# The chunked layer's preparation in a fixed order, with two blocks of its convolution on the tensor engine

## The chip, the core and the metric

The kernel runs on one core of a Trainium2 chip. A core has five engines that take their instructions from queues of their own: PE (TensorE: matrix products), DVE (VectorE), ACT (ScalarE) and POOL (GpSimd) for element-wise work, and SP (SyncE), which here only issues DMAs. PE writes to PSUM, a small memory that DVE and ACT read; everything else works on SBUF. The metric is the device time of one launch in microseconds (us); lower is better.

## The reference

Eight images of 64 x 64 x 96 in fp32 pass through four layers, each as `x = x + layer(group_norm(x))`. Layers 0 and 2 are selective scans, layer 3 upsamples, transforms and filters spectrally, and layer 1, which the change concerns, is a scan in chunks:

```python
xz = x @ in_proj_w.T                       # 96 -> 2 x 192
xi, z = split(xz)
u = silu(depthwise_conv3x3(xi, conv_w) + conv_b)
xs = cross_scan(u)                         # k = 0: by rows, 1: by columns, 2 and 3: both reversed
dt_raw, B, C = split(x_proj_w[k] @ xs[k])  # 6 + 16 + 16 rows for each direction k
dt = softplus(dt_raw + dt_bias[k])
# for each chunk of positions: decays exp(cumsum(dt * A)), C.B within the chunk, a state between chunks
y = cross_merge(scan(xs, dt, A, B, C, D))
x_out = layernorm(y) * silu(z) @ out_proj_w.T
```

The 192 channels of u are the six heads of 32; the scan needs, for every position, u with positions on the partitions, dt, B in two layouts and C.

## The kernel before

The loop over images (line 1566) runs, for each image, group norm, the input projection and the layer's own function for layers 0, 1 and 2; `back` (line 303) does the gate, norm and output projection of one layer at the start of the next. The spectral layer of an image is executed in small pieces beside the next image's two selective scans, and for the last image alone at the end. No such pieces run beside the chunked layer.

Activations have channels on the partitions: `y` (the projection's output) and `u` (after convolution and silu) are 96 x 2 halves x 4096 positions.

`chunked_scan` (line 1036) loads the layer's constants and calls `chunked_order` (line 1072) twice: with `o = 0` for the directions 0 and 2 (positions row by row) and with `o = 1` for 1 and 3 (column by column). Each call has two parts. The second part is a loop over 32 chunks of 128 positions in both directions (lines 1172 to 1422), written under `tc.manual_schedule()`: the order in the program is the order in each engine's queue. The first part is the preparation (lines 1086 to 1170). It has no such mark, so a list scheduler orders its instructions on each engine by their dependencies. It consists of:

- for `o = 0` alone, the convolution. Seven of the eight blocks of eight rows are done on DVE (`conv`, line 275: nine taps, lines 280 and 282), in portions of rows 0-16, 16-32, 32-48 and 48-56, each for two halves of the channels; block 7 is done on PE with diagonal matrices (`conv_pe`, line 291, matrices made by POOL in `diagonals`). Each portion ends with ACT's activation (`silu`, line 296), which writes `u`.
- `pr`: the B and C rows for all positions (line 1117). One tile holds four groups of 512 positions for one direction; there are four tiles. DVE copies each from PSUM to `bcs` (line 1125) and four DMAs of SP's queue write it to DRAM (`bcd`, line 1128), from where the loop's `quad` reads it back as `bt` and `cr` for four chunks at a time.
- for each of 32 chunks, a tile `pt` (three PSUM buffers): two matmuls, one for each half of the channels, give the transposed u of that half and the half's share of two directions' dt rows and B rows (line 1143). With `o = 1` a chunk's positions lie 64 elements apart, and each half is first copied together into `uc` (four buffers): half 0 by POOL (line 1137), half 1 by ACT (line 1138). The transposed u goes to `xt` (line 1144), by ACT in even and by DVE in odd chunks; ACT copies half 0's 44 small columns to `xd` (line 1148) and DVE adds those of half 1 (line 1149).
- at the end, for all chunks together: dt with its bias (line 1153), softplus (line 1158), the decays' factors `lw` and the ends of chunks (to line 1170).

The loop's first instructions on DVE include a memset of a PSUM tile, `pst2` (line 1186).

Of the kernel before, what the change touches and what calls it, by code (L numbers as in the profile page):

```python
# [9 lines left out]
F32 = mybir.dt.float32  # L10
# [7 lines left out]
DM = 96  # L18
NST = 16
RK = 6  # L20
# [7 lines left out]
Q = 128  # L28
NQ = L // Q
# [38 lines left out]
def tile_vision_stack(  # L68
# [19 lines left out]
    nc = tc.nc  # L88
# [60 lines left out]
    with (  # L149
# [6 lines left out]
        for i, (dtw, dtx, w) in enumerate(((dt0, dx0, w0), (dt2, dx2, w2))):  # L156
# [12 lines left out]
            for k in range(K):  # L169
                pw = pp.tile([DM, 2, 192], F32, name="pw", bufs=2)  # L170
                for hf in range(2):
# [4 lines left out]
                        start=True,  # L176
                        stop=True,
# [12 lines left out]
        for m in range(3):  # L190
            pt = pp.tile([128, DM], F32, name="pt")
# [71 lines left out]
    def taps(y, rows, hf, acc):  # L263

        at, end = rows
        av = acc.rearrange("p (r c) -> p r c", c=64)
        xv = y[:, hf, :].rearrange("p (r c) -> p r c", c=64)
        for tap in (4, 0, 1, 2, 3, 5, 6, 7, 8):
            dy, dx = tap // 3 - 1, tap % 3 - 1
            r0, r1 = max(at, -dy), min(end, 64 - dy)  # L270
            c0, c1 = max(0, -dx), min(64, 64 - dx)
            src = xv[:, r0 + dy : r1 + dy, c0 + dx : c1 + dx]
            yield tap, src, av[:, r0 - at : r1 - at, c0:c1]

    def conv(w, y, u, rows, hf):
        out = u[:, hf, rows[0] * 64 : rows[1] * 64]
        for tap, src, dst in taps(y, rows, hf, out):
            cw = w[:, C_CW + hf * 9 + tap : C_CW + hf * 9 + tap + 1]
            if tap == 4:
                nc.vector.tensor_scalar_mul(dst, src, cw)  # L280
            else:
                nc.vector.scalar_tensor_tensor(dst, src, cw, dst, ALU.mult, ALU.add)
        silu(w, u, rows, hf, out)

    def diagonals(dg, w):
        for n in range(18):
            nc.gpsimd.tensor_scalar_mul(
                dg[:, n, :], ident[:DM, :DM], w[:, C_CW + n : C_CW + n + 1]
            )

    def conv_pe(dg, y, j, hf, acc):
        for tap, src, dst in taps(y, (8 * j, 8 * j + 8), hf, acc):
            nc.tensor.matmul(dst, dg[:, 9 * hf + tap, :], src, start=(tap == 4), stop=(tap == 8))

    def silu(w, u, rows, hf, acc):
        nc.scalar.activation(
            u[:, hf, rows[0] * 64 : rows[1] * 64],
            acc,
            AF.Silu,
            bias=w[:, C_CB + hf : C_CB + hf + 1],  # L300
        )
# [119 lines left out]
    def view(t, wh, at, n):  # L421

        if not wh:
            return t[:, at : at + n]
        return t.rearrange("p (h w) -> p w h", w=64)[:, at // 64 : (at + n) // 64, :]

    def cut(t, wh):

        return t.rearrange("p (w h) -> p w h", h=64) if wh else t
# [260 lines left out]
    def selective_scan(w, wdt, a, d, u, y, beside):  # L690
# [23 lines left out]
        with (  # L714
# [14 lines left out]
            def prepare(i):  # L729

                k, c = steps[i]
                wh, at = k % 2 == 1, c * LC
                uv = [view(u[:, hf, :], wh, at, LC) for hf in range(2)]
                m = made[i] = {"dx": [], "du": []}
                if i in (0, 2, NCH + 2, 2 * NCH + 2):
# [336 lines left out]
    def chunked_order(o, w, d, xproj, u, y, yr, cc, lw, bts, crs, bcds, op):  # L1072
# [8 lines left out]
        xt = op.tile([128, NQ, 192], F32, name="xt")  # L1081
        xd = op.tile([128, NQ, 2, RK + NST], F32, name="xd")
        dt = op.tile([128, NQ, 2, RK], F32, name="dt")
        TX = DM + 2 * (RK + NST)
        d_end = op.tile([128, NQ, 2, RK], F32, name="d_end")
        with (
            tc.tile_pool(name="turn", bufs=2) as cp,
            tc.tile_pool(name="pt", bufs=3, space=PSUM) as ptp,
            tc.tile_pool(name="pc", bufs=1, space=PSUM) as pcp,
            tc.tile_pool(name="pr", bufs=2, space=PSUM) as prp,  # L1090
            tc.tile_pool(name="acc", bufs=2, space=PSUM) as acp,
        ):
            if o == 0:
                dg = cp.tile([DM, 18, DM], F32, name="dg", bufs=1)
                diagonals(dg, w)
                for rows in ((0, 16), (16, 32), (32, 48), (48, 56)):
                    for hf in range(2):
                        conv(w, y, u, rows, hf)
                for hf in range(2):
                    acc = acp.tile([DM, 512], F32, name="acc")  # L1100
                    conv_pe(dg, y, 7, hf, acc)
                    silu(w, u, (56, 64), hf, acc)
            tx = cp.tile([DM, 2, TX], F32, name="tx", bufs=1)
            for hf in range(2):
                nc.gpsimd.tensor_copy(tx[:, hf, :DM], ident[:DM, :DM])
                nc.gpsimd.tensor_copy(
                    tx[:, hf, DM:].rearrange("p (i r) -> p i r", i=2),
                    xproj[:, o::2, hf, : RK + NST],
                )

            for j in range(2):
                for i in range(2):
                    k = o + 2 * i
                    pr = prp.tile([128, 4 * Q], F32, name="pr")
                    for hf in range(2):
                        for g in range(4):
                            nc.tensor.matmul(
                                pr[32 * g : 32 * g + 32, :],
                                xproj[:, k, hf, RK:XR],
                                view(u[:, hf, :], o == 1, (4 * j + g) * 4 * Q, 4 * Q),  # L1120
                                start=(hf == 0),
                                stop=(hf == 1),
                            )
                    bcs = cp.tile([128, 4 * Q], F32, name="bcs")
                    nc.vector.tensor_copy(bcs, pr)
                    for g in range(4):
                        at = (4 * j + g) * 4 * Q
                        nc.sync.dma_start(
                            bcds[k][:, at : at + 4 * Q], bcs[32 * g : 32 * g + 32, :]
                        )  # L1130
            for c in range(NQ):
                if o == 0:
                    uv = [u[:, hf, c * Q : (c + 1) * Q] for hf in range(2)]
                else:

                    uc = cp.tile([DM, 2, Q], F32, name="uc", bufs=4)
                    nc.gpsimd.tensor_copy(cut(uc[:, 0, :], True), view(u[:, 0, :], True, c * Q, Q))
                    nc.scalar.copy(cut(uc[:, 1, :], True), view(u[:, 1, :], True, c * Q, Q))
                    uv = [uc[:, hf, :] for hf in range(2)]

                pt = ptp.tile([128, 2, TX], F32, name="pt")
                for hf in range(2):
                    nc.tensor.matmul(pt[:, hf, :], uv[hf], tx[:, hf, :], start=True, stop=True)
                (nc.vector.tensor_copy if c % 2 else nc.scalar.copy)(
                    xt[:, c, :].rearrange("p (j m) -> p j m", j=2), pt[:, :, :DM]
                )
                xdc = xd[:, c, :, :].rearrange("p i r -> p (i r)")
                nc.scalar.copy(xdc, pt[:, 0, DM:])
                nc.vector.tensor_add(xdc, xdc, pt[:, 1, DM:])
            for i in range(2):  # L1150
                k = o + 2 * i
                bias = r1s[:, k * RK : (k + 1) * RK]
                nc.vector.tensor_add(
                    dt[:, :, i, :],
                    xd[:, :, i, 0:RK],
                    bias.unsqueeze(1).to_broadcast([128, NQ, RK]),
                )
            nc.scalar.activation(dt, dt, AF.Softplus)
            for i in range(2):
                k = o + 2 * i  # L1160
                a = r1s[:, 24 + k * RK : 24 + (k + 1) * RK]
                dt_a = lw[:, i, :, RK : 2 * RK]
                nc.vector.tensor_mul(
                    dt_a, dt[:, :, i, :], a.unsqueeze(1).to_broadcast([128, NQ, RK])
                )

                pe = pcp.tile([128, NQ, RK], F32, name="pe")
                nc.tensor.matmul(pe, past[i], dt_a, start=True, stop=True)
                nc.scalar.activation(d_end[:, :, i, :], pe, AF.Exp)
            nc.vector.tensor_mul(d_end, d_end, dt)  # L1170
# [395 lines left out]
    for b in range(batch):  # L1566
        xd = xp.tile([DM, L], F32, name="xd")
# [7 lines left out]
        with tc.tile_pool(name="layers", bufs=1) as uyp:  # L1575
            u = uyp.tile([DM, 2, L], F32, name="u")
            y = uyp.tile([DM, 2, L], F32, name="y")
            stats = uyp.tile([DM, 8, 6], F32, name="stats")
            sbs = [uyp.tile([DM, 2], F32, name=f"sb{n}") for n in range(3)] + [sb3]
            for n in range(4):  # L1580
                with (
# [3 lines left out]
                    if n == 0:  # L1585
                        wi = columns(rp, w0, W_IN, 192, "wi")
                        xs = rp.tile([DM, L], F32, name="xs")
                        with (
# [11 lines left out]
                            for j in range(8):  # L1600
                                pt = pp.tile([DM, 4, 128], F32, name="pt")
# [170 lines left out]
```

## Time and profile before

| | us |
|---|---|
| median of 3 runs | 27056.74 |
| lowest and highest | 27053.37, 27074.89 |
| profiled execution, its own time | 27082.74 |
| its span on the core | 27080.9 |
| DVE busy in the span | 23966.2 (88%) |
| PE busy | 22624.0 (84%) |
| POOL busy | 21781.7 (80%) |
| ACT busy | 16539.7 (61%) |
| first preparation of image 0, from the projection's first matmul to line 1153 | 1400.46 to 1505.91 |
| second preparation of image 0, from its first matmul to line 1153 | 1701.19 to 1736.84 |

Times in the profile count from the start of the span. A row of the timeline gives start and duration, the engine, the line, the operation, what it writes and reads, partitions x elements, how many instructions the row holds together, and in brackets how long the engine had been idle and what released it. A matmul in fp32 shows as two records. PEclk is the share of the full clock that the tensor engine was granted.

### The profile page before, as it was taken

To read this page: it belongs to the slowest core of one execution; us is meant where nothing else is said; L and a number is where in the kernel's file an instruction comes from. 1 tells how busy PE (TensorE), PEld (TensorE's weight loads), DVE (VectorE), ACT (ScalarE), POOL (GpSimd) and SP (SyncE) were. 2 spreads that over 40 slices of the span, in tenths; PEclk is the share of its full clock that TensorE was granted. 3 is DMA by queue.
4 is the path that set the end of the run, shared out by engine and by line. 5 is a ranking of instruction groups with operands and counts; after the bars stand their busy time and mean duration, and the time that the engine had idled before them with its cause. 6 is when DMAs were issued, how large, how long until landed. Compare 5 with 4: busy or idle time off the path is not lost. (4 is left out here: it accounts for less than half of the span.)

```text
span 27080.9 us, 283056 instructions
## 1 busy us (share of the span) xinstructions
PE 22624.0 (84%) x91061; PEld 8150.5 (30%) x91061; DVE 23966.2 (88%) x17105; ACT 16539.7 (61%) x29953; POOL 21781.7 (80%) x8360
## 2 busy tenths in 40 slices
PE   7787788888888888888888888888888888888888
PEld 2141122422224222242222422224222342223424
DVE  8989899798997989979898898988989889898896
ACT  5656566466665656556565565655656556565564
POOL 8949898498984979859797697976979769797694
PEclk7687777877778777787777877778777787778878
DMA  4415454154541545415453254532545325453252
GB/s 121 119 30 124 114 130 117 31 131 122 132 111 35 133 117 137 103 44 132 116 136 98 50 132 118 135 92 56 133 119 134 85 62 133 118 134 78 70 133 67
DMA packets 1681704, 2831.72 MB, mean 105 GB/s; under 512 B 434984, under 2 KB 478280, under 8 KB 1675616
## 3 DMA queue, kind: packets, MB, share of 16 engines
q1 hardware_dynamic: 1663584, 2807.32, 41.9%
q8 instruction: 730, 11.96, 0.2%
q10 hardware_dynamic: 16640, 6.29, 0.1%
q14 instruction: 750, 6.14, 0.1%
HBM read 2385.11 MB, written 427.49 MB: 104 GB/s over the span
## 5 line engine op out<-in xcount | busy, mean ns | idle before, releaser
L870 DVE TENSOR_TENSOR_SCAN h<-da,db 128x1026 f32<-128x1026 f32 x6144 | 13765.8, 2282 | 900.6 <-ACT da L855 479.2
L891 POOL TENSOR_TENSOR h<-h,c 128x2048 f32<-128x2048 f32 x3072 | 12769.4, 4174 | 726.0 <-ACT state L886 510.1
L908 PE MATMUL py<-h,cst 128*32 128x512 f32 x24576 | 5301.4, 795 | 69.9 <-POOL h L891 69.8
L855 ACT ACTIVATE da<-dx,a2s 128x512 f32<-128x512 f32 x6144 | 4236.4, 690 | 1508.7 <-DVE h L870 1366.6
L855 ACT ACTIVATE da<-dx,a0s 128x512 f32<-128x512 f32 x6144 | 4235.8, 690 | 1481.8 <-DVE h L870 1344.3
L840 POOL TENSOR_TENSOR db<-du,b 128x2048 f32<-128x2048 f32 x1024 | 4648.2, 4539 | 567.6 <-ACT db L826 567.6
L840 DVE TENSOR_TENSOR db<-pu,b 128x2048 f32<-128x2048 f32 x2048 | 4643.9, 2268 | 110.9 <-PE pu L834 100.6
L834 PE MATMUL pu<-du,cst 32*128 32x512 f32 x4096 | 3239.2, 881 | 1007.4 <-DVE db L840 799.9
L908 PEld LDWEIGHTS py<-h,cst 128*32 128x32 f32 x24576 | 1175.0, 142 | 4827.3 <-issue 4517.4
L751 PE MATMUL pv<-u,wk 96*128 96x512 f32 x2048 | 1816.9, 1030 | 688.4 <-ACT raw L747 685.8
L898 PE MATMUL py<-y,cst 96*96 96x512 f32 x1536 | 1517.0, 1084 | 397.9 <-ACT raw L755 395.4
L834 PEld LDWEIGHTS pu<-du,cst 32*128 32x128 f32 x4096 | 790.4, 239 | 3079.7 <-issue 1361.9
L742 PE MATMUL pv<-u,wk 96*96 96x512 f32 x2048 | 1452.4, 838 | 186.7 <-ACT y L993 142.6
L1285 ACT ACTIVATE sg<-sg 128x768 f32<-128x768 f32 x1024 | 819.6, 800 | 859.1 <-PE sg L1269 859.1
L993 ACT COPY y<-py 96x512 f32<-96x512 f32 x512 | 417.5, 815 | 1411.4 <-PE py L908 1411.4
L516 PE MATMUL ps<-s,w3as 96*128 96x512 f32 x1344 | 912.4, 767 | 327.7 <-ACT sf L523 188.1
L1239 POOL TENSOR_TENSOR ce<-ec,cr 112x512 f32<-112x512 f32 x256 | 530.8, 2074 | 719.1 <-ACT ec L1237 700.8
L1317 DVE TENSOR_TENSOR wt<-wt,cbm 128x768 f32<-128x768 f32 x1024 | 985.3, 997 | 136.6 <-ACT wt L1286 136.1
L886 ACT COPY state<-h 128x4 f32<-128x4 f32 x3072 | 597.5, 194 | 782.5 <-DVE h L870 776.8
L751 PEld LDWEIGHTS pv<-u,wk 96*128 96x128 f32 x2048 | 540.6, 291 | 1740.2 <-ACT raw L747 1212.5
L319 POOL TENSOR_SCALAR xn<-xs,sb 96x512 f32<-96x512 f32 x192 | 198.1, 1033 | 991.7 <-PE pz L324 495.6
L1216 POOL TENSOR_TENSOR rr<-lr,cc 128x768 f32<-128x768 f32 x256 | 376.6, 1471 | 754.1 <-ACT lr L1214 749.2
(241 smaller groups left out, 30790.9 us busy)
## 6 DMA issues: line engine op xcount, KB each, us to landing
dx<-dd SPq DMA_DIRECT2D x4096, 192.0 KB
b<-bcd SPq DMA_DIRECT2D x2048, 256.0 KB
c<-bcd SPq DMA_DIRECT2D x2048, 256.0 KB
du<-dud SPq DMA_DIRECT2D x2048, 128.0 KB
dd<-raw SPq DMA_DIRECT2D x1024, 192.0 KB
dud<-du SPq DMA_DIRECT2D x512, 128.0 KB
xd<-xs SPq DMA_DIRECT2D x256, 192.0 KB
cr<-bcd SPq DMA_DIRECT2D x1536, 32.0 KB
```

Source lines behind the costliest of these rows:

```text
L516: nc.tensor.matmul(ps, w3as[:, m * 128 : (m + 1) * 128], live["x2"], start=True, stop=True)
L742: nc.tensor.matmul(pv[:DM], weights[k][:, hi, 128:], uv[hi], start=(hi == 0), stop=(hi == 1))
L751: nc.tensor.matmul(pv, weights[k][:, hi, :128], uv[hi], start=(hi == 0), stop=(hi == 1))
L834: nc.tensor.matmul(pu, sel[rows, :], m["du"][rows, n // 3, :], start=True, stop=True)
L840: (nc.gpsimd if pool else nc.vector).tensor_mul(groups(m["db", n]), (m["du2"][:, n // 3, :] if pool else m["pu"]) .unsqueeze(1) .to_broadc ...
L855: nc.scalar.activation(dst[:, g, :LC], made[i]["dx"][n // 3][:, n % 3, :], AF.Exp, scale=av4[:, k, n, gs : gs + 1],)
L870: nc.vector.tensor_tensor_scan(made[i]["h", n][:, at][:, way], das[p][:, rev : 2 * SEG + rev][:, way], made[i]["db", n][:, at][:, way], 0. ...
L891: nc.gpsimd.tensor_mul(h, h, made[i]["c"])
L898: nc.tensor.matmul(py, skip[:, hf, :] if k == 0 else ident[:DM, :DM], view((u if k == 0 else y)[:, hf, :], wh, c * LC, LC), start=True, st ...
L908: nc.tensor.matmul(py[32 * q : 32 * q + 32, :], red, hs[q][:, g, :], start=False, stop=(g == NSG - 1),)
L1285: nc.scalar.activation(sg, sg, AF.Abs)
L1317: nc.vector.tensor_mul(it["wt"], it["wt"], m["cbm"][:, j : j + 1, :].to_broadcast([128, RK, Q]),)
```

## The change

Both preparations come under `tc.manual_schedule()`, and their parts become functions that are called in a written order.

- `on_dve` convolves a portion of 16 rows on DVE, `on_pe` a block of eight rows on PE. DVE now does the blocks 0 to 5, PE the blocks 6 and 7.
- `share(j)` is half of `pr` (two tiles, one for each direction of the order), `tokens(at, end)` the transposes of a range of chunks, and `join(at, end)` the addition of the two halves' small columns for a range of chunks.
- For `o = 0` the transposes of a portion stand behind that portion's activation. For `o = 1` the first half of `pr` comes first, then eight chunks, the other half of `pr`, and the remaining chunks by eights.
- ACT copies the small columns of both halves in one instruction (128 x 88) to a new tile `both`; DVE's 32 additions become additions over 8 or 16 chunks.
- The copies to `xt` are all on ACT with `o = 0` and all on DVE with `o = 1`; the copies to `bcs` are on ACT with `o = 0`, on DVE with `o = 1`.
- With `o = 1`, `pr` reads `u` with eight neighbouring elements innermost (`near`), and the copy to `bcs` puts the positions back in the order of columns (`turn_back`).

```diff
--- before.py
+++ after.py
@@ -423,6 +423,16 @@
         if not wh:
             return t[:, at : at + n]
         return t.rearrange("p (h w) -> p w h", w=64)[:, at // 64 : (at + n) // 64, :]
+
+    def near(t, wh, at, n):
+
+        if not wh:
+            return t[:, at : at + n]
+        return t.rearrange("p (h w) -> p h w", w=64)[:, :, at // 64 : (at + n) // 64]
+
+    def turn_back(t, wh, n):
+
+        return t.rearrange("p (h w) -> p w h", w=n // 64) if wh else t
 
     def cut(t, wh):
 
@@ -1089,17 +1099,11 @@
             tc.tile_pool(name="pc", bufs=1, space=PSUM) as pcp,
             tc.tile_pool(name="pr", bufs=2, space=PSUM) as prp,
             tc.tile_pool(name="acc", bufs=2, space=PSUM) as acp,
+            tc.manual_schedule(),
         ):
             if o == 0:
                 dg = cp.tile([DM, 18, DM], F32, name="dg", bufs=1)
                 diagonals(dg, w)
-                for rows in ((0, 16), (16, 32), (32, 48), (48, 56)):
-                    for hf in range(2):
-                        conv(w, y, u, rows, hf)
-                for hf in range(2):
-                    acc = acp.tile([DM, 512], F32, name="acc")
-                    conv_pe(dg, y, 7, hf, acc)
-                    silu(w, u, (56, 64), hf, acc)
             tx = cp.tile([DM, 2, TX], F32, name="tx", bufs=1)
             for hf in range(2):
                 nc.gpsimd.tensor_copy(tx[:, hf, :DM], ident[:DM, :DM])
@@ -1107,8 +1111,21 @@
                     tx[:, hf, DM:].rearrange("p (i r) -> p i r", i=2),
                     xproj[:, o::2, hf, : RK + NST],
                 )
-
-            for j in range(2):
+            both = cp.tile([128, NQ, 2, 2 * (RK + NST)], F32, name="both", bufs=1)
+
+            def on_dve(at, end):
+                for hf in range(2):
+                    conv(w, y, u, (at, end), hf)
+
+            def on_pe(n):
+                accs = []
+                for hf in range(2):
+                    accs.append(acp.tile([DM, 512], F32, name="acc"))
+                    conv_pe(dg, y, n, hf, accs[hf])
+                for hf in range(2):
+                    silu(w, u, (8 * n, 8 * n + 8), hf, accs[hf])
+
+            def share(j):
                 for i in range(2):
                     k = o + 2 * i
                     pr = prp.tile([128, 4 * Q], F32, name="pr")
@@ -1117,36 +1134,73 @@
                             nc.tensor.matmul(
                                 pr[32 * g : 32 * g + 32, :],
                                 xproj[:, k, hf, RK:XR],
-                                view(u[:, hf, :], o == 1, (4 * j + g) * 4 * Q, 4 * Q),
+                                near(u[:, hf, :], o == 1, (4 * j + g) * 4 * Q, 4 * Q),
                                 start=(hf == 0),
                                 stop=(hf == 1),
                             )
                     bcs = cp.tile([128, 4 * Q], F32, name="bcs")
-                    nc.vector.tensor_copy(bcs, pr)
+                    (nc.vector.tensor_copy if o else nc.scalar.copy)(
+                        cut(bcs, o == 1), turn_back(pr, o == 1, 4 * Q)
+                    )
                     for g in range(4):
                         at = (4 * j + g) * 4 * Q
                         nc.sync.dma_start(
                             bcds[k][:, at : at + 4 * Q], bcs[32 * g : 32 * g + 32, :]
                         )
-            for c in range(NQ):
-                if o == 0:
-                    uv = [u[:, hf, c * Q : (c + 1) * Q] for hf in range(2)]
-                else:
-
-                    uc = cp.tile([DM, 2, Q], F32, name="uc", bufs=4)
-                    nc.gpsimd.tensor_copy(cut(uc[:, 0, :], True), view(u[:, 0, :], True, c * Q, Q))
-                    nc.scalar.copy(cut(uc[:, 1, :], True), view(u[:, 1, :], True, c * Q, Q))
-                    uv = [uc[:, hf, :] for hf in range(2)]
-
-                pt = ptp.tile([128, 2, TX], F32, name="pt")
-                for hf in range(2):
-                    nc.tensor.matmul(pt[:, hf, :], uv[hf], tx[:, hf, :], start=True, stop=True)
-                (nc.vector.tensor_copy if c % 2 else nc.scalar.copy)(
-                    xt[:, c, :].rearrange("p (j m) -> p j m", j=2), pt[:, :, :DM]
-                )
-                xdc = xd[:, c, :, :].rearrange("p i r -> p (i r)")
-                nc.scalar.copy(xdc, pt[:, 0, DM:])
-                nc.vector.tensor_add(xdc, xdc, pt[:, 1, DM:])
+
+            def tokens(at, end):
+                for c in range(at, end):
+                    if o == 0:
+                        uv = [u[:, hf, c * Q : (c + 1) * Q] for hf in range(2)]
+                    else:
+
+                        uc = cp.tile([DM, 2, Q], F32, name="uc", bufs=4)
+                        nc.gpsimd.tensor_copy(
+                            cut(uc[:, 0, :], True), view(u[:, 0, :], True, c * Q, Q)
+                        )
+                        nc.scalar.copy(cut(uc[:, 1, :], True), view(u[:, 1, :], True, c * Q, Q))
+                        uv = [uc[:, hf, :] for hf in range(2)]
+
+                    pt = ptp.tile([128, 2, TX], F32, name="pt")
+                    for hf in range(2):
+                        nc.tensor.matmul(
+                            pt[:, hf, :], uv[hf], tx[:, hf, :], start=True, stop=True
+                        )
+                    (nc.vector.tensor_copy if o else nc.scalar.copy)(
+                        xt[:, c, :].rearrange("p (j m) -> p j m", j=2), pt[:, :, :DM]
+                    )
+                    nc.scalar.copy(both[:, c], pt[:, :, DM:])
+
+            def join(at, end):
+                nc.vector.tensor_add(
+                    xd[:, at:end].rearrange("p c i r -> p c (i r)"),
+                    both[:, at:end, 0, :],
+                    both[:, at:end, 1, :],
+                )
+
+            if o == 0:
+                on_dve(0, 16)
+                on_pe(6)
+                tokens(0, 8)
+                on_dve(16, 32)
+                on_pe(7)
+                share(0)
+                tokens(8, 16)
+                tokens(24, 32)
+                on_dve(32, 48)
+                join(0, 16)
+                join(24, 32)
+                share(1)
+                tokens(16, 24)
+                join(16, 24)
+            else:
+                share(0)
+                tokens(0, 8)
+                share(1)
+                for at in (8, 16, 24):
+                    tokens(at, at + 8)
+                    join(at - 8, at)
+                join(24, 32)
             for i in range(2):
                 k = o + 2 * i
                 bias = r1s[:, k * RK : (k + 1) * RK]
```

## The prediction

> **What bounds the kernel now.** I read the page first, for the shares and the costliest groups.
>
> ```profile
> PE 22624.0 (84%) x91061; PEld 8150.5 (30%) x91061; DVE 23966.2 (88%) x17105; ACT 16539.7 (61%) x29953; POOL 21781.7 (80%) x8360
> L870 DVE TENSOR_TENSOR_SCAN h<-da,db 128x1026 f32<-128x1026 f32 x6144 | 13765.8, 2282 | 900.6 <-ACT da L855 479.2
> ```
>
> DVE is busiest, and over half of its time is line 870: the two selective scans bound the kernel, and the change does not touch them. It touches the preparations of the chunked layer, two per image. In the timeline the first runs from image 0's projection (1400.46 us) to its dt additions (1505.91), the second from the first transposes (1701.19) to 1736.84. In all eight images the first takes 105.5 to 106.3 us and pr to dt in the second 34.4 to 34.6, so image 0 stands for all. No neighbouring work fills them, so what they gain or lose goes into the end.
>
> The table of windows (busy us of PE, PEld, DVE, ACT, POOL, then the granted TensorE clock) shows what limits each stretch:
>
> ```profile
> core 0: us, PE busy (x) PEld busy (x) DVE busy (x) ACT busy (x) POOL busy (x), PEclk, DMA share, GB/s
> 1460.00:1480.00 20.00, 0.00 (x0) 0.00 (x0) 20.00 (x25) 2.55 (x3) 0.00 (x0) 0.50 0.00 0
> 1480.00:1500.00 20.00, 17.52 (x116) 12.03 (x116) 11.39 (x42) 6.81 (x33) 0.00 (x0) 0.88 0.29 76
> 1709.00:1712.00 3.00, 3.00 (x20) 0.59 (x16) 0.69 (x1) 0.00 (x0) 0.00 (x0) 1.00 0.25 66
> 1720.00:1736.00 16.00, 14.19 (x101) 12.55 (x100) 8.25 (x41) 13.69 (x62) 9.62 (x23) 1.00 0.19 46
> ```
>
> At 1460 DVE convolves and PE waits for it; then PE does everything that depends on u. In the second preparation PE is full, first with pr alone, then with the transposes.
>
> Last the timeline, for durations and for who releases whom:
>
> ```profile
> 1472.42 7.94 DVE L282 SCALAR_TENSOR_TENSOR u<-y,w1s,u 96x504 f32<-96x504 f32 x12
> 1481.08 0.23 PEld L1117 LDWEIGHTS pr<-u,xproj 96*32 96x32 f32 x8 [25.98 <-ACT u L296]
> 1505.91 0.63 DVE L1153 TENSOR_TENSOR dt<-xd,r1s 128x192 f32<-128x192 f32 x2
> 1701.19 1.30 PE L1143 MATMUL pt<-tx,uc 96*128 96x140 f32 x4 [1.26 <-POOL uc L1137]
> 1702.42 13.94 PE L1117 MATMUL pr<-u,xproj 96*32 96x512 f32 x64
> 1717.07 0.36 DVE L1144 COPY xt<-pt 128x192 f32<-128x192 f32 x1 [3.39 <-PE pt L1143]
> 1717.13 0.47 ACT L1138 COPY uc<-u 96x128 f32<-96x128 f32 x1 [13.83 <-PE pt L1143]
> 1717.94 0.78 ACT L1138 COPY uc<-u 96x128 f32<-96x128 f32 x2
> 1735.54 0.30 ACT L1148 COPY xd<-pt 128x44 f32<-128x44 f32 x2
> 1736.38 0.20 ACT L1148 COPY xd<-pt 128x44 f32<-128x44 f32 x1 [0.55 <-DVE xt L1144]
> 1736.84 0.63 DVE L1153 TENSOR_TENSOR dt<-xd,r1s 128x192 f32<-128x192 f32 x2
> ```
>
> The uc copies come in pairs, ahead of the xd copies: the planner lets the transposes' inputs run ahead. And an xd copy waits for DVE's xt copy of the same PSUM tile. Both matter below.
>
> **First preparation: a gain.** DVE loses one block of rows, two halves of 5.7 us; PE takes it. Chain after, on image 0's clock:
> - PE: block 6 after the projection, 14.9 us as block 7 took (1417.3 to 1432.1), then eight chunks, block 7, share(0), sixteen chunks: done by about 1465 and waiting for DVE again.
> - DVE: rows 0-16 done at 1427.4 and 16-32 at 1447.7 as now, rows 32-48 another 20.26. In the order of the built program the later loop's memset of pst2 (line 1186, 0.48 us) stands inside these taps, and waits for the activation of block 7, whose PSUM it takes over, at about 1453.2: DVE had got there at 1450.7, so 2.5 us stall. Queued behind it are the rest of the taps, so it counts in full. Ends 1470.9.
> - Activation 1.15 us: 1472.1. The rest of share(1), 12 matmuls: 5.2 us if all at half clock (0.86 us for each two, as in 1481 to 1484), 2.6 at full; I take 4.5, since PE comes out of an idle stretch. 1476.7. The bcs copy, and eight chunks at 0.55 us (four passes of 0.14): 1481.3. Copy, addition: dt at 1482.6.
>
> Gain 1505.9 - 1482.6 = 23.3 us. Bounds: 26 without the stall and with PE at full clock, 19 with the chunks at today's 0.63 and a longer wait. The sixteen DMAs of bcd on SP's queue are issued as before; the last bcs copy at 1477.5 puts the quads' loads at about 1485.7, where the first cb matmul wants them at 1485.9: cover just enough, 2 us of risk if the activations are late. The 32 additions of 128x44 (0.18 to 0.20 us) that become two of 128x352 and one larger lie beside PE's work: 0. The constants on POOL stand as they stood: 0.
>
> **Second preparation: a loss.** pr with the nearer read: eight contiguous elements instead of a stride of 64. Before, a group of four matmuls takes 0.857 us (13.94/16 = 0.87 with the ends), the first ones at half clock and the later ones at full alike; the first preparation's contiguous reads take 0.43 at full clock (after 1484) and 0.86 at half. So each share gains nothing at half clock and 3.4 us at full.
>
> The transposes cost more. In program order ACT's queue holds uc(0), both(0), uc(1), both(1) and so on. both(c) needs chunk c's second matmul, and waits for DVE's xt(c). Queued behind it is uc(c+1), which chunk c+1's second matmul needs, for which xt(c+1) waits. Nothing runs ahead: one closed ring per chunk where the planner had pairs. A turn, from rows at full clock: uc 0.43; to PE's first pass 0.12; the second half's two passes from a stop 0.51; hand-over to DVE 0.04, xt 0.35; to ACT 0.03; both, till the next copy may start, 0.13 (88 columns, between 0.09 for 44 and 0.22 for 192). Sum 1.60 us, against 0.637 now. At half clock the pair takes 0.84 (first pair after 1701.19, clock 0.50): 1.93 us.
>
> Which clock? These rows decide:
>
> ```profile
> 1380.00:1400.00 20.00, 11.57 (x19) 3.43 (x17) 14.47 (x27) 1.65 (x3) 10.63 (x21) 0.65 0.16 49
> 1448.00:1452.00 4.00, 3.45 (x16) 0.40 (x10) 4.00 (x5) 0.00 (x0) 0.00 (x0) 0.50 0.00 0
> 1516.00:1520.00 4.00, 2.60 (x13) 1.79 (x14) 0.52 (x1) 0.92 (x2) 3.50 (x7) 0.88 0.23 59
> 1520.00:1524.00 4.00, 4.00 (x37) 2.38 (x35) 2.25 (x4) 3.00 (x5) 1.21 (x1) 0.70 0.01 3
> ```
>
> PE busy 58 to 65% of a stretch lost the full clock, and at half clock 86% for 4 us did not win it back. The ring keeps PE busy about 0.8 of 1.60 us, 50%, or 1.4 of 1.93, 74%, below those rows on both counts: it should fall to half and stay. I take 1.93, and keep 1.60 as the other end.
>
> "TensorE: Matmul & The Clock Gate", section "HAM oscillation", gives as its abstract rule that PE must have no gap over about 3.4 us. By that alone, gaps under 1 us would keep the full clock, and the sum below would be 25 us instead of 38. The trace disagrees: between 1381 and 1389 no gap exceeds 2.01 us, and the clock fell.
>
> Sum: share(0) starts at 1700.8 and lasts 6.9 us at half clock; chunk 1's uc at about 1708.9; six turns to uc(7); 1.4 to the end of chunk 7's pair (0.43 + 0.12 + 0.84), where PE's order has share(1), 6.5 long; uc(8) is copied meanwhile, so 1.3 more to uc(9) (0.84 + 0.04 + 0.35 + 0.03); 22 turns to uc(31); 1.8 to its both, and 0.7 for that and the last addition. That is 1720.5 + 28 turns: 1774.5 at 1.93. Loss 1774.5 - 1736.8 = 37.7 us. At 1.60, with share(1) at 3.4: 1762.2, loss 25.4. The two DVE copies per share that undo the order of pr are 0.69 us each if the strided read costs nothing; twice that adds under 1.4 to a share's end, mostly beside PE's work: 0 to 1.4, and I take 0. DVE's bcs copies wait for pr, and queued behind them are only xt copies whose chunks PE issues after pr: 0. bcd's DMAs are issued by about 1730 and the quads' loads have 40 us: 0. All xt on DVE leaves it under a third busy, and the few additions lie beside the ring: 0.
>
> Net +14.4 us per image, 8 x 14.4 = 115. The profiled execution took 27082.74 us (span 27080.9, and 1.8 around it), 26 above the median of 27056.74; added to the median: 27172.
>
> **Rivals.** (1) The ring keeps full clock: net 25.4 - 23.3 = +2.1, with the first preparation's bounds -0.6 to +6.4 per image: 27052 to 27108. For it: 1480 to 1484 won the clock back after 2.9 us busy of 4. Against it: the rows above.
>
> (2) Faster, by one mechanism: ACT's queue does not hold the next uc copy, because both(c) leaves early or a turn is much shorter. It decides at a turn of (1736.8 + 23.3 - 1720.5)/28 = 1.41 us, or 1.52 if share(1) runs at full clock. At 1.3 the second preparation ends at 1756.9, or 3 earlier: net -3.2 to -6.3, 27031 to 27006; if chunks keep 0.637 and pr loses nothing, -23.3 per image, 26870; with pr's 6.9 gained too, 26815. For it: 13.69 of 16 us of ACT is busy now, and the new queue has less work. Against it: 1736.38, where the copy did wait for DVE's xt.
>
> (3) The first preparation gains only 10, since activations queue behind the copies of sixteen chunks on ACT, and loads come late: net +27, 27275. Against it: these copies are done by 1465, before rows 32-48.
>
> **How the numbers follow.** Runs differ by some 0.1%; I call 0.2% (54 us, 6.8 per image) what can be told. The forecast case has 0.66: its own range, from the bounds 19 and 26 and a turn of 1.85 to 2.0, is +9 to +21 per image, 27130 to 27225. Rival 1 has 0.15, within 54 us. Rival 2 has 0.13, a third of it above 26990. Rival 3 has 0.06. Slower 0.72, same 0.15, faster 0.13. The range 26990 to 27235 leaves out most of rivals 2 and 3.
>
> **What would show it.** In the changed profile: uc copies on ACT in the second preparation singly, 1.9 us apart, PEclk 0.50 through it, dt additions some 74 us after the loop's last addition to y, where they came 36 after. In the first: PE busy with block 6 up to 1432, DVE's taps ending near 1471, dt additions some 82 us after the projection began. uc copies nearer than 1.4 us overturn the forecast; PEclk of 1.00 between shares makes it rival 1; a first preparation over 95 us makes it rival 3.

## The result and the profile after

The changed kernel takes 27221.42 us (median of 4 runs, 27206.65 to 27238.82) where the kernel before took 27065.82 in the same comparison (median of 4, 27053.37 to 27079.69): 1.0058 times as long, 95% interval 1.004 to 1.0075. The profiled execution took 27238.82 us.

The page shows what it showed before: the scans of layers 0 and 2 are where they were (their line is now 880).

```profile
PE 22895.0 (84%) x91349; PEld 8326.0 (31%) x91349; DVE 23864.7 (88%) x16473; ACT 16586.9 (61%) x29985; POOL 21717.3 (80%) x8360
...
L880 DVE TENSOR_TENSOR_SCAN h<-da,db 128x1026 f32<-128x1026 f32 x6144 | 13764.6, 2282 | 899.1 <-ACT da L865 478.1
```

The answer lies in the two preparations. I divided the chunked layer of each image at instructions that both traces have: the projection's first matmul, the dt additions of the two preparations, and the last addition to y of the two loops. Means over the eight images, in us:

| | before | after |
|---|---|---|
| first preparation | 106.0 | 89.0 |
| first loop | 196.0 | 195.7 |
| second preparation | 36.1 | 69.1 |
| second loop | 190.0 | 192.2 |
| sum | 528.0 | 546.0 |

The first preparation gives 17.0 us and the second takes 33.0. Eight images make 8 x 18.0 = 144 of the 156 us between the two spans (27236.7 - 27080.9). No experiment was made on the second loop's 2.2 us or on the 12 us outside the chunked layer; runs of one kernel differ by as much. One thing differs in the trace: from 20 to 60 us into the second loop the tensor engine had less than the full clock (0.82 to 0.92) in five of after's eight images and in one of before's. Whether this makes the 2.2 us is not shown.

The windows of after (busy us of PE, PEld, DVE, ACT, POOL, then PEclk; PEld is PE loading the weights of a matmul), two from the first preparation and two from the second:

```profile
core 0: us, PE busy (x) PEld busy (x) DVE busy (x) ACT busy (x) POOL busy (x), PEclk, DMA share, GB/s
1468.00:1477.00 9.00, 1.38 (x8) 0.00 (x0) 8.79 (x8) 0.00 (x0) 0.00 (x0) 0.51 0.00 0
1478.00:1488.00 10.00, 8.59 (x56) 4.86 (x56) 0.85 (x3) 5.64 (x20) 0.00 (x0) 0.81 0.23 57
1692.00:1696.00 4.00, 1.75 (x10) 1.34 (x11) 0.79 (x3) 1.60 (x6) 0.93 (x3) 1.00 0.25 66
1716.00:1748.00 32.00, 22.68 (x71) 16.67 (x70) 7.47 (x20) 9.09 (x35) 6.26 (x16) 0.50 0.04 9
```

The shape of the first preparation is as before, only shorter: DVE alone with its taps, then PE with what was left. In the second no engine is full any more. PE is the busiest with 71% of 32 us, at half clock, and DVE, ACT and POOL stand at 20 to 28%.

The timeline of after, first preparation:

```profile
1466.58 10.40 DVE L282 SCALAR_TENSOR_TENSOR u<-y,w1s,u 96x1008 f32<-96x1008 f32 x8
...
1478.22 4.58 PE L1134 MATMUL pr<-u,xproj 96*32 96x512 f32 x24 [8.83 <-ACT u L296]
...
1482.73 4.08 PE L1166 MATMUL pt<-tx,u 96*128 96x140 f32 x32
...
1487.89 0.63 DVE L1207 TENSOR_TENSOR dt<-xd,r1s 128x192 f32<-128x192 f32 x2
```

And second, two turns:

```profile
1718.53 0.40 ACT L1161 COPY uc<-u 96x128 f32<-96x128 f32 x1
1718.99 0.96 PEld L1166 LDWEIGHTS pt<-tx,uc 96*128 96x128 f32 x4 [0.88 <-ACT uc L1161]
...
1719.86 0.36 DVE L1169 COPY xt<-pt 128x192 f32<-128x192 f32 x1 [1.49 <-PE pt L1166]
...
1720.25 0.23 ACT L1172 COPY both<-pt 128x88 f32<-128x88 f32 x1 [1.31 <-DVE xt L1169]
1720.38 0.40 ACT L1161 COPY uc<-u 96x128 f32<-96x128 f32 x1
1720.83 0.97 PEld L1166 LDWEIGHTS pt<-tx,uc 96*128 96x128 f32 x4 [0.88 <-ACT uc L1161]
```

Each row names the one ahead of it as its releaser, across three engines and back: uc on ACT releases PE, PE releases xt on DVE, xt releases both on ACT, and uc follows in ACT's own queue. That is a ring. From one uc copy to the next it takes 1.85 us.

### The profile page after: what moved, and what is told of

It is laid out like the page before. It is cut to its first block, busy times and chain, and to the rows that moved or that the text cites. A ratio compares the mean times of both kernels' runs of the same rounds, so it can differ in the third digit from the quotient of the medians.

```text
span 27236.7 us, 282904 instructions
## 1 busy us (share of the span) xinstructions
PE 22895.0 (84%) x91349; PEld 8326.0 (31%) x91349; DVE 23864.7 (88%) x16473; ACT 16586.9 (61%) x29985; POOL 21717.3 (80%) x8360
```

## The experiments

e1 to e5 start from the changed kernel, e6 to e8 from e5's. "First" and "second" are the preparations, means over eight images; the ratio is to the kernel before on the same chip.

| kernel | ratio, 95% interval | first, us | second, us |
|---|---|---|---|
| before | 1 | 106.0 | 36.1 |
| after | 1.0058 (1.004 to 1.0075) | 89.0 | 69.1 |
| e1: uc two chunks ahead | 0.9919 (0.9905 to 0.9934) | 88.9 | 28.5 |
| e2: taps alternate | 1.0032 (1.002 to 1.0043) | 81.6 | 69.1 |
| e3: second preparation planned | 0.9939 (0.9925 to 0.9954) | 89.2 | 31.6 |
| e4: ring with PE kept busy | 1.0013 (1.0004 to 1.0023) | 89.2 | 59.2 |
| e5: e1 and e2 | 0.9898 (0.9883 to 0.9913) | 81.5 | 28.0 |
| e6: e5 with the strided read | 0.9913 (0.9899 to 0.9928) | 81.5 | 32.6 |
| e7: e5 with seven blocks on DVE | 0.9931 (0.9915 to 0.9948) | 94.8 | 28.1 |
| e8: e5 with one addition per chunk | 0.9906 (0.9891 to 0.9921) | 81.2 | 30.9 |

**e1, the ring opened.** `gather` holds the two uc copies of a chunk, as they stood in `tokens`:

```diff
-                        uc = cp.tile([DM, 2, Q], F32, name="uc", bufs=4)
-                        nc.gpsimd.tensor_copy(
...
+                        while len(ucs) < min(c + 3, NQ):
+                            gather(len(ucs))
+                        uv = [ucs[c][:, hf, :] for hf in range(2)]
```

> Edit: in the second preparation of the changed kernel the two uc copies of a chunk are issued two chunks earlier in the program; nothing else moves. Theory (a ring through ACT's queue: uc, PE, xt on DVE, both, next uc): the ring then spans three chunks, a turn falls from 1.52 to 1.85 us to some 0.6 to 0.7, the preparation from 69 us to 33 to 38, the kernel by 31 to 36 us per image, 250 to 290 us, to about 26935 to 26975. Rival A (the time is in the hand-over from PE to DVE to ACT within each chunk, with all xt copies on DVE): a turn stays above 1.2 us, and the kernel gains under 100 us. Rival B (the time is in the half clock): a turn stays at 1.5 or above unless the clock is full, the kernel gains under 80 us.

Measured: 26861.94 us, 359 less than after, with the second preparation 40.6 us shorter; both are more than the theory asked. The timeline of e1:

```profile
1699.09 12.94 PE L1170 MATMUL pt<-tx,uc 96*128 96x140 f32 x96
...
1701.79 0.23 ACT L1176 COPY both<-pt 128x88 f32<-128x88 f32 x1
1701.92 0.42 ACT L1156 COPY uc<-u 96x128 f32<-96x128 f32 x1
1702.27 0.23 ACT L1176 COPY both<-pt 128x88 f32<-128x88 f32 x1
1702.40 0.41 ACT L1156 COPY uc<-u 96x128 f32<-96x128 f32 x1
```

Same instructions on ACT in the same alternation, mostly 0.48 us apart, and in this stretch with no wait before them. PE does 24 chunks in 12.94 us without a stop, 0.54 each. The hand-overs between engines within a chunk are still there, and so are the xt copies on DVE: rival A is out. Rival B is not answered here, since PE, busy for 9.87 of the 10 us from 1701, had the full clock; e4 answers it. The Trainium skill, "TensorE: Matmul & The Clock Gate", section "Architectural detail", says that ACT and DVE take their queues strictly in order, while PE's queue may pull weight loads ahead. e1 agrees for ACT: a turn of 1.52 us at full clock (1.85 at half) became 0.54 by an earlier place in ACT's queue alone.

**e3, the order left to the planner** (the list scheduler), for the second preparation only:

```diff
...
-            tc.manual_schedule(),
+            tc.manual_schedule() if o == 0 else nullcontext(),
```

> Edit: the changed kernel's second preparation alone without the fixed order, same operations, so that the list scheduler orders it; the first preparation is as changed. Theory (the fixed order is what closes the ring): uc copies are hoisted, a chunk takes 0.6 to 0.75 us again, the preparation falls from 69 us to 31 to 37, the kernel by 32 to 38 us per image, 255 to 300 us, to about 26920 to 26965. Rival A (the larger copies of both halves and all xt copies on DVE cost the time, whatever the order): the preparation stays above 50 us, and the kernel gains under 150 us.

Measured: 26915.91 us, 306 less than after, a little more than expected; second preparation 31.6. The timeline of e3 has uc copies ahead of the both copies again:

```profile
1691.29 0.95 ACT L1161 COPY uc<-u 96x128 f32<-96x128 f32 x2 [5.65 <-PE pt L1166]
1692.14 0.35 ACT L1172 COPY both<-pt 128x88 f32<-128x88 f32 x2
```

So it was the written order that closed the ring. The changed operations themselves are worth something: under the same planner 31.6 us against 36.1 before. A written order that runs ahead (e1) beats the planner by 3.1.

**e4, the clock's share.** Between the matmuls of a chunk's two halves PE does one more, whose result nobody reads:

```diff
+                        if o == 1 and hf == 1:
+                            nc.tensor.matmul(
+                                spare[:, :256], ident[:DM, :DM], u[:, 0, :256], start=True, stop=True
+                            )
...
+            if o == 1:
+                spare = acp.tile([DM, 512], F32, name="acc")
```

> Edit: in the second preparation of the changed kernel, PE does one matmul more per chunk (96x256, its result unused) between the matmuls of the two halves, in time in which it waits for uc; it keeps PE busy. Theory (a busy share of PE of some 50 to 75% drops the clock to half, and that costs 0.33 us of each turn): PEclk stays near 1.00, every turn is 1.52 us, and the preparation falls from 69 us to about 58 to 62, the kernel by 55 to 90 us, to about 27140. The ring itself stays: no turn below 1.45. Rival (the busy share does not decide the clock, or the extra matmul lies on the ring): turns of 1.85 us or above, and the kernel is no faster.

Measured: 27115.98 us, 105 less than after, second preparation 59.2. A window of e4, and two uc copies in a row:

```profile
1712.00:1736.00 24.00, 18.46 (x96) 11.95 (x96) 6.59 (x18) 8.38 (x32) 5.52 (x14) 1.00 0.02 6
...
1721.11 0.40 ACT L1161 COPY uc<-u 96x128 f32<-96x128 f32 x1
...
1722.63 0.40 ACT L1161 COPY uc<-u 96x128 f32<-96x128 f32 x1
```

In image 0 all turns but those that span a share take 1.52 or 1.53 us, and PEclk stays 1.00 through them. More work made the kernel faster: the half clock's price is the 0.33 us between 1.52 and 1.85, some 10 us per image, or 80 for the kernel, as expected. The other 25 of the 105 lie outside this preparation: the second loop's mean is 189.4 against after's 192.2, for a reason that is not shown. The remaining 31 us of the preparation down to e1 are the ring's own.

**e2, the taps.** `on_dve` takes the taps of both halves in turn:

```diff
-                    conv(w, y, u, (at, end), hf)
+                pairs = zip(*(taps(y, (at, end), hf, outs[hf]) for hf in range(2)))
+                for pair in pairs:
+                    for hf, (tap, src, dst) in enumerate(pair):
...
```

> Edit: in the changed kernel, on_dve issues the taps of the two halves alternately instead of one half after the other; the activations of both halves follow. Theory (a tap that adds to the result of the tap just before it starts 0.04 to 0.10 us after that one's end, where a tap on the other half starts 0.075 before it): taps come every 1.18 us instead of every 1.30, 48 taps save 5.8 us per image, the later activation of half 0 gives up to 1 us back, the first preparation falls from 89 to 83.5 to 85 us, the kernel by 32 to 46 us, to about 27180. Rival (taps are slowed by what PE, ACT and POOL read and write beside them, since PE now works through this stretch): the distance stays at 1.30 us, and the kernel within 10 us.

Measured: 27165.79 us, 56 less than after, first preparation 7.5 us shorter; the theory had 32 to 46 and 4 to 5.5. The timelines of before, after and e2, each a run of taps with start and total time:

```profile
1435.85 4.81 DVE L282 SCALAR_TENSOR_TENSOR u<-y,w1s,u 96x1008 f32<-96x1008 f32 x4
```

```profile
1432.77 9.17 DVE L282 SCALAR_TENSOR_TENSOR u<-y,w1s,u 96x1008 f32<-96x1008 f32 x7
```

```profile
1429.69 10.72 DVE L1125 SCALAR_TENSOR_TENSOR u<-y,w1s,u 96x1008 f32<-96x1008 f32 x9
```

With the last tap (1.25 to 1.27 us) taken off, the starts are 3.56/3 = 1.19 us apart before, 7.90/6 = 1.32 after, and 9.47/8 = 1.18 in e2. PE and ACT are as busy beside the taps in e2 (100% and 35% from 1430 to 1451) as in after (99% and 31% from 1432 to 1454), so the rival, a slowdown by the neighbours, is out. What differs is what the tap ahead wrote: after adds to the result of the tap just before it, e2 and before to the other half's. The planner had woven the two halves before; nothing in the text of that kernel says so. 48 taps at 0.133 make 6.4 us; in the mean of the images the taps ended 6.0 us earlier, with `pst2`'s memset (0.5 us) now behind them. The other 1.5 of the 7.5 us lie between the last tap and the dt additions: in e2 the last eight chunks took 4.1 us in every image, in after 6.1 in seven of eight, at a granted clock of 1.00 against 0.66.

**e5, both mended.**

> Edit: the uc copies two chunks ahead and the alternating taps, both together in the changed kernel. Theory (the two losses are independent and lie in different preparations): the gains add up. Per image 89.0 - 7.5 for the first preparation (81.5) and 28.5 for the second, against 106.0 and 36.1 before: 32 us per image less than before, 255 to 275 us, to about 26805. Rival (an earlier end of one preparation runs into late loads of bt and cr): 30 us or more of this are lost in the loops.

Measured: 26832.06 us, 0.9898 of the kernel before, the lowest median here; 281 less than before on the same chip (27112.92), where 255 to 275 was expected. The two preparations take 109.5 us together, 32.7 less than before: the gains add. The loops' means are 198.4 and 190.1 against 196.0 and 190.0, 20 us over eight images, less than the rival's 30; e6, which is the same up to the end of the first loop, has 196.3 there, so most of this is the spread between executions. The loads cost little: the first cb matmul came 4.4 us after the dt additions began, 3.9 in before.

**e6, the read of pr.** In e5's kernel:

```diff
-                                near(u[:, hf, :], o == 1, (4 * j + g) * 4 * Q, 4 * Q),
+                                view(u[:, hf, :], o == 1, (4 * j + g) * 4 * Q, 4 * Q),
...
-                        cut(bcs, o == 1), turn_back(pr, o == 1, 4 * Q)
+                        bcs, pr
```

> Edit: in e5's kernel, pr of the second preparation reads u with a stride of 64 elements, and its copy keeps the order, as the kernel before did. Theory (the nearer read pays where PE has the full clock): the two shares take 6.9 us each instead of 5.6 and 3.6, the second preparation is 4 to 5 us longer, the kernel 30 to 40 us slower than e5. Rival (hidden beside the copies): within 10 us of e5.

Measured: 26875.22 us, 43 above e5, second preparation 4.6 us longer, as expected. The timelines of e5 and e6:

```profile
1673.90 5.50 PE L1143 MATMUL pr<-u,xproj 96*32 96x512 f32 x32 [0.94 <-DVE y L1464]
...
1683.61 3.64 PE L1143 MATMUL pr<-u,xproj 96*32 96x512 f32 x32
```

```profile
1674.70 7.08 PE L1143 MATMUL pr<-u,xproj 96*32 96x512 f32 x32 [0.94 <-DVE y L1464]
...
1685.99 7.05 PE L1143 MATMUL pr<-u,xproj 96*32 96x512 f32 x32
```

The strided read takes 7.1 us per share, in the first, where PEclk is 0.50 for the first half and 0.91 for the second, as in the second, at 1.00 throughout. The nearer one takes 3.6 at full clock and 5.5 where it starts at half.

**e7, one block back on DVE.** `on_pe(6)` goes, `on_dve(48, 56)` follows `on_dve(32, 48)`, and chunks 24 to 27 move behind the second share.

> Edit: in e5's kernel, DVE convolves rows 48 to 56 too, after rows 32 to 48, PE block 7 alone; the chunks of those rows move behind the second share. Theory (DVE's taps are the chain of the first preparation): 18 taps at 0.65 us, 11.8 us, and four chunks more behind them, 2 us: 12 to 14 us per image, 95 to 110 us slower than e5. Rival (the order alone made the gain and PE's block merely moved work): within 30 us of e5.

Measured: 26912.51 us, first preparation 13.3 us longer, as expected; but the kernel is 80 us slower than e5, not 95 to 110. The first loop's mean is 194.6 against e5's 198.4, and why is not shown. DVE's taps are the chain of the first preparation, and the block on PE is worth what DVE would have spent on it.

**e8, small additions** in e5's kernel, at the same places:

```diff
-                nc.vector.tensor_add(
-                    xd[:, at:end].rearrange("p c i r -> p c (i r)"),
...
+                for c in range(at, end):
+                    nc.vector.tensor_add(
+                        xd[:, c].rearrange("p i r -> p (i r)"), both[:, c, 0, :], both[:, c, 1, :]
+                    )
```

> Edit: in e5's kernel, each of the additions over 8 or 16 chunks becomes one addition per chunk, at the same place in the program. Theory (additions lie beside other work but for the last eight of each preparation): 0.5 to 1 us per preparation, 5 to 15 us for the kernel. Rival (32 additions hold up DVE's queue): over 30 us.

Measured: 26852.51 us, 20 above e5 with overlapping ranges of runs; so the kernel's time does not settle it. The second preparation is 2.9 us longer, more than the 0.5 to 1 of the theory. A join in e5, then in e8:

```profile
1691.77 0.61 DVE L1188 TENSOR_TENSOR xd<-both 128x352 f32<-128x352 f32 x1
```

```profile
1690.52 1.50 DVE L1189 TENSOR_TENSOR xd<-both 128x44 f32<-128x44 f32 x8
```

0.9 us more, three times, in DVE's queue: twice ahead of xt copies for which ACT waits, and once ahead of the dt additions. With the ring open DVE is near the path, and the few larger additions are worth some 3 us there.

## Why the prediction was right

Forecast 27172 with 27130 to 27225 as the likeliest case's own range; measured 27221, against a median before of 27066 in this comparison. The forecast difference was 115, the measured one 156.

The direction and the mechanism held, but the total came out nearer than its parts, and that is luck. Per image the first preparation gave 6.3 us less than forecast and the second took 4.7 less; the two misses nearly cancel, to +16.0 where +14.4 was forecast. Of the 156 us these 16.0 make 128; the other 28, in the loops and outside the layer, had no term in the sum.

- **The second preparation's ring** is what the trace shows, link by link, and e1 and e3 confirm it. Its size was 33.0 us instead of 37.7. In image 0 a turn took 1.85 us and not 1.93 at half clock, 1.52 and not 1.60 at full: from the start of a uc copy to PE 0.46 and not 0.55, the other steps within 0.01. That makes 28 turns of 49.9 us in all instead of 54.0, with six of them (three after each share) at or near the full clock. The second share, with the steps around it, was 1.3 us shorter than taken, since the clock rose within it. In three of the eight images the full clock lasted for fewer turns, and the preparation took 70.4 to 71.4 us instead of 68.0 to 68.1.
- **The clock** fell as the rows said, after a PE busy share of 44% of the four us at 1692, and stayed down at 71%. Rival 1 is out; e4 is close to the kernel that it described, and stands 39 us above before in the medians, where rival 1 had it at -5 to +51.
- **The rule on gaps** that the prediction set against these rows, from the Trainium skill's "TensorE: Matmul & The Clock Gate", section "HAM oscillation", is that PE must have no gap over about 3.4 us. Keeping to it was not enough here: in image 0 PE's stops in the ring at full clock were 0.78 to 0.84 us, and the full clock was lost after the fourth chunk. e4 kept it with the same ring, with stops of 0.34 us and a higher busy share; which of the two decides is not shown.
- **The first preparation** gave 17.0 us instead of 23.3, below the lower bound of 19. Two terms were wrong. One is "rows 32-48 another 20.26", and the same pace for rows 0-16 and 16-32: it carried the distance between taps of a woven order into an order that is not woven. To this comes a misreading: 1427.4, taken as the end of rows 0-16, is where the first tap of the next rows started, with two taps of rows 0-16 (2.4 us) still to come; ACT's activation of their second half started at 1431.75. In image 0 the taps ended at 1477.0, not 1470.9, although the stall at the memset fell away. The order of the built program shows the taps unwoven; the prediction took the memset from it, and not the distances.
- **PE's clock behind the taps** is the other term. In image 0 it was as taken (share(1) 4.58 us against 4.5, eight chunks 4.08 against 4.4). In the other seven images share(1) ran at half clock throughout and the chunks partly so; in image 1 the stretch from the last tap to the chunks and then the chunks (columns as in the windows above):

```profile
4823.12:4829.63 6.51, 5.28 (x24) 0.99 (x24) 1.23 (x2) 1.73 (x2) 0.00 (x0) 0.50 0.15 40
4829.63:4835.73 6.10, 6.10 (x36) 5.89 (x32) 0.00 (x0) 3.75 (x15) 0.00 (x0) 0.66 0.23 59
```

In the mean the taps ended 5.2 us later after the projection's start than forecast, and 13.4 us passed from there to the dt additions where 11.7 were taken. Image 0 stood for all before the change, as the prediction says, but not after it.
- **The memset's stall** of 2.5 us did not come: DVE reached it at 1457.7, when the activation of block 7 had just ended (1456.7), and it cost 0.1 and its own 0.5. DVE was 7.0 us later than taken, the activation 3.5.
- **Cover of the loads** was enough: in the mean the first cb matmul began 3.5 us after the dt additions had begun, where it was 3.9 before. Image 0 alone would have misled here (4.4 against 3.3).
- **The additions at 0** were not tested with the ring in place; e8 shows that without the ring they are worth 2.9 us in the second preparation, and nothing in the first (81.2 against 81.5).

Rivals 2 and 3 are out: no uc copies came nearer than 1.52 us, and the first preparation gained 17.

## What to carry to other kernels

An order written by hand takes over everything that the planner did unseen: here copies that ran ahead by pairs, and taps of two independent halves that were woven. Before writing one, list for each engine which instructions of the next round stand ahead of which of this round, and follow every queue round until it closes; a turn's length is then a sum of rows. When a duration is carried from one order to another, look whether it was a distance between dependent or independent instructions. And where one image is to stand for eight, look at its clock in the others too.

## What the runs showed of the hardware that I had not expected

On DVE a tap that adds to the result of the instruction just ahead starts 0.035 to 0.10 us after its end; a tap on other data starts 0.075 before it. For instructions of 1.25 us that is 10%. One matmul more per chunk made the kernel 105 us faster: with PE busy for 77% of the time and stops of 0.34 us it kept the full clock; at 44% and stops of 0.78 us it had lost it, and at 71% of the time at half clock it did not win it back. The strided fp32 read of 64 elements' distance takes 7.1 us per share, whether the share starts at half clock or runs at full clock throughout, about the 6.9 us that the nearer one was taken to need at half (8 x 0.86).
